# Places of tokens in extra sets worked out after the first list, and the last results loaded together on two queues

## The chip, the cores and the metric

The kernel runs on one core of one Trainium2 chip. The metric is the device time of one execution in microseconds (us). A core has five engines with an instruction stream each: PE (matrix products; its weight loads are shown as PEld), DVE (vector), ACT (activations), POOL (general, it also issues the indirect transfers) and SP (it issues most plain transfers). Data moves between HBM and the core's memory by DMA queues.

## What is computed

3125 tokens of 256 numbers and 50000 directed edges, sorted by their target, go through two layers, each a graph step and a mixture of experts. In each mixture every token goes to its two best experts of eight.

```python
# layer 1, graph: own features and those of the last edge into the node
agg = zeros_like(x).at[dst].set(x[src])
x = x + concat((xn, agg)) @ W.T + b          # xn: layernorm of x
# layer 1, experts: top 2 of 8, hidden size 1024
x = x + sum_over_two(weight_i * (relu(xn @ W1[e].T + b1[e]) @ W2[e].T + b2[e]))
# layer 2, graph: over all edges
msg = (t1[src] + (feat[src] * feat[dst]) @ W2) / sqrt(out_deg[src] * out_deg[dst])   # feat: layernorm of x, t1 = feat @ W1
x = x + unit_norm(leaky_relu(t1 + segment_sum(msg, dst)))     # 0 + ... for nodes with no edge in
# layer 2, experts: top 2 of 8, hidden size 256
x = x + xn + sum_over_two(weight_i * (gelu(xn @ w1[e] + b1[e]) @ w2[e] + b2[e]))
```

A token's two weights are the softmax over its two scores.

## The kernel before

Tokens lie in 25 tiles of 128 rows (the last holds 53), in two halves: tiles 0 to 13 and 14 to 24. X in the core's memory holds all of them.

**Routing.** `route_steps` (L649 to L777) is a generator: each `yield` hands the turn back to whatever it runs beside. It ranks a token's eight scores, marks the best and the two selected experts, and counts by two matmuls (L685, L686) how many tokens of each expert come before. From the counts it makes each token's place in its experts' list. An expert has a fixed set of tiles per half, with room for 488 or 368 tokens. A token over the room is given a place in an "extra set" further back: `extrai`, `extras`, `last` and `away` (L708 to L723) hold how many extra sets each expert needs and how far a place has to move, `past` (L731) marks the places over the room, and L735/L736 add `past` times `away`. Then r.at holds each token's two places (L740 to L745). The extra sets are used only in a branch that runs if some expert overflows.

`list_steps` (L779 to L863) turns places into lists: one-hot matrices `lane` and `col` on DVE, two passes of matmuls (L812) that count into PSUM, and from these `take` (which row to fetch) and `put` (where its result goes). Behind the list `route_steps` makes the two weights of each token (L759 to L776).

**Experts.** `experts` (L940 to L1088) goes through 16 sets, eight experts for each half. For one set: hidden chunks by matmuls into PSUM tile `big` (L1045) with an activation on ACT (L1049); then `turn` transposes the rows of the next set, gathered from a table by POOL (L999), into PSUM tile `tr`, of which there are two buffers (L1018), and DVE copies them out as `xs` (L1019); then the second matmuls into `y` (L1059), DVE adds the bias (L1064), and POOL scatters the result to `ytab` (L1068). Between these `slot()` gives one step to each generator of the list `beside`. The order of instructions on every engine is that in which this code issues them, under a manual schedule; so the number of yields in a generator sets where its work stands in each engine's order.

The route of the first half in layer 1 runs before the first `experts` call, beside the last of the graph step (`plus_own`). That of the second half runs inside it: `beside_first` (L1420) runs the rest of the graph step, the ranks, `route_steps(routed1[1], ...)`, then `windows` (L1137 to L1218) and `total_in`, `count_edges` (L1238), clears of tables, and the combine of the first half. `windows` finds where each tile's edges start: POOL numbers positions (L1144), DVE compares (`less`, L1153), PE counts (L1159), POOL fetches seven pieces `win` (L1168), a chain on DVE works on them (L1177 to L1208: `code`, `qf`, `same`, `into`), PE transposes `qf` and `code` into `tr` (L1216), and ACT copies them out as `qs` and `cs` (L1217).

**The end.** In layer 2 the results of the first half are loaded and combined beside the second half's sets (`beside_fourth`, L1764). For the second half, `one_result` loads result 0 or result 1 of groups of three tiles, all on SP's queue (L1747, L1751). Result 0 is loaded during the last set: the loads are declared free of the last set's scatters (`apart`), since in this half a token's result 0 is that of its lower-numbered expert, and the last expert's results are always result 1. Result 1 is loaded behind the last scatter. A combine is one DVE instruction for each tile and result (L1799), 11 of each; a group is stored as soon as its result 1 is added (`store`, L1118, on SP).

Of the kernel before, what the change touches and what calls it, by code (L numbers as in the profile page):

```python
# [8 lines left out]
F32 = mybir.dt.float32  # L9
F16 = mybir.dt.float16  # L10
BF16 = mybir.dt.bfloat16
I32 = mybir.dt.int32
AF = mybir.ActivationFunctionType
OP = mybir.AluOpType
# [86 lines left out]
def gnn_ffn_kernel(ctx: ExitStack, tc: tile.TileContext, x, src_a, src_d, dst_d, dst_row,  # L101
# [547 lines left out]
    def route_steps(r, rp, h, pl, layer, sc=None):  # L649
# [55 lines left out]
        nc.vector.tensor_scalar(stop, shift, room - 0.5, None, OP.add)  # L705
        nc.vector.tensor_sub(shift[:, 1:], shift[:, 1:], ends[:, :NE - 1])
        yield
        extrai = rp.tile([P, NE], I32, name="extrai")  # L708
        nc.vector.tensor_scalar(extrai, many, -room, 0.0, OP.add, OP.max)
        nc.vector.tensor_scalar(extrai, extrai, SX * P - 1, None, OP.add)  # L710
        nc.vector.tensor_scalar(extrai, extrai, (SX * P).bit_length() - 1, None, OP.arith_shift_right)
        if layer == 2:
            yield
        extras = rp.tile([P, NE], F32, name="extras")
        nc.vector.tensor_copy(extras, extrai)
        r.last = keep.tile([P, NE], F32, tag=f"last{layer}{h}", name="last")
        nc.vector.tensor_tensor_scan(r.last, ones_f[:, :NE], extras, 0.0, OP.mult, OP.add)
        r.over = r.last[0:1, NE - 1:]
        yield
        away = rp.tile([P, NE], F32, name="away")  # L720
        nc.vector.tensor_sub(away, r.last, extras)
        nc.vector.tensor_scalar(away, away, float(SX * P), FIXED[h] * P - 0.5, OP.mult, OP.add)
        nc.vector.tensor_sub(away, away, stop)  # L723
        if layer == 2:
            yield
        place = rp.tile([P, NE, n], F32, name="place")
        nc.vector.tensor_sub(place.rearrange("p e t -> p (e t)"), flat, count)
        nc.vector.tensor_add(place, place, pp[:, 0])
        yield
        nc.vector.tensor_add(place, place, shift[:, :, None].to_broadcast([P, NE, n]))  # L730
        past = rp.tile([P, NE, n], F32, name="past")  # L731
        nc.vector.tensor_tensor(past, place, stop[:, :, None].to_broadcast([P, NE, n]), OP.is_gt)
        if layer == 2:
            yield
        nc.vector.tensor_mul(past, past, away[:, :, None].to_broadcast([P, NE, n]))  # L735
        nc.vector.tensor_add(place, place, past)  # L736

        one = [best, rp.tile([P, n, NE], F32, name="second")]
        nc.vector.tensor_sub(one[1], sel, best)
        r.at = keep.tile([P, 2, n], F32, tag=f"at{layer}{h}", name="at")  # L740
        for i in range(2):
            yield
            got = rp.tile([P, n, NE], F32, name="got")
            nc.vector.tensor_mul(got, one[i], place.rearrange("p e t -> p t e"))
            nc.vector.tensor_reduce(r.at[:, i, :], got, AX.X, OP.add)  # L745
        yield

        r.weight = keep.tile([P, 2, n], F32, tag=f"weight{layer}{h}", name="weight")
        if t1 == T:
            none = rp.tile([P, 1], F32, name="none")  # L750
            nc.vector.tensor_scalar(none, real, -float(1 << 15), float(1 << 15), OP.mult, OP.add)
            nc.vector.tensor_scalar(r.at[:, :, n - 1], r.at[:, :, n - 1], none, None, OP.add)
        if not r.adds:
            yield from list_steps(r, rp, h, layer, 0, FIXED[h])
        if not softmax_first:
            sc.exps()
            yield
            yield
# [178 lines left out]
            nc.sync.dma_start(out=b2t, in_=b2[e, :].to_broadcast([P, D]))  # L937
            got += [w2, b2t]

    def experts(fp, sets, routed, tabs, weights, nh, act, beside=(), fresh=False, loaded=None, now=None,  # L940
                apart=None):


        lead = 2 if nh > 2 else 3
# [78 lines left out]
        with tc.manual_schedule(engines=ENGINES):  # L1023
# [10 lines left out]
            for k, (h, e, x) in enumerate(sets):  # L1034
# [20 lines left out]
                for j in range(n):  # L1055
                    m = last_rows if j == n - 1 else P
                    py = bank([P, D], F32, "y")
                    for c in range(nh):
                        nc.tensor.matmul(py[:m], hid[:, c, j * P:j * P + m], w2[:, c, :],  # L1059
                                         start=(c == 0), stop=(c == nh - 1))  # L1060
                        if c % 2 and c < nh - 1:
                            slot()
                    y = fp.tile([P, D], F32, name="y", bufs=4 if nh > 2 else 10)
                    nc.vector.tensor_add(y[:m], py[:m], b2t[:m])  # L1064
                    to = routed[h].column(c0 + j)
                    into = bass.IndirectOffsetOnAxis(ap=to[1][:m], axis=0)
                    if not routed[h].adds:
                        dma = nc.gpsimd.indirect_dma_start(  # L1068
                            out=tabs[h][1], out_offset=into, in_=y[:m], in_offset=None,
                            bounds_check=2 * tokens(h) - 1, oob_is_err=False)  # L1070
                        alone(dma, tabs[h][1], fresh)
                        if apart and k == len(sets) - 1:
                            tc.declare_no_dep(dma.ins, group=apart, reason="other rows")
                    else:

                        nc.scalar.activation(y[:m], y[:m], AF.Identity, scale=to[2][:m])
                        dma = nc.gpsimd.indirect_dma_start(
                            out=out, out_offset=into, in_=y[:m], in_offset=None,
                            bounds_check=N - 1, compute_op=OP.add)
                        tc.declare_no_dep(dma.ins, group=sums_of(h, e, x), reason="other rows")  # L1080
                        tc.add_to_no_dep_group(sums_of(h, e, x), dma.ins)
                    if nh > 2 or j % 2:
                        take(1)
                    slot()
# [30 lines left out]
            for t in range(t0, t1):  # L1115
                combine(h, r.weight_x if over else r.weight, y2, t0, t)

    def store(t0, t1):  # L1118
        whole = min(t1, T - 1)
        if whole > t0:  # L1120
            nc.sync.dma_start(out=out[t0 * P:whole * P, :].rearrange("(t p) d -> p t d", p=P), in_=X[:, t0:whole, :])
        if t1 == T:
            nc.sync.dma_start(out=out[(T - 1) * P:, :], in_=X[:LAST, T - 1, :])

# [439 lines left out]
    def to_the_end():  # L1566
# [171 lines left out]
            with tc.tile_pool(name="route3", bufs=1, reuse_waits="tile") as rp:  # L1738
                yield from route_steps(routed2[1], rp, 1, None, 2, state["scores"])

        def one_result(pool, t0, t1, i):

            first = HALVES[1][0]
            y1 = pool.tile([P, t1 - t0, D], F32, name=f"result{i}_{t0}")
            whole = min(t1, T - 1)
            ytab = tabs2[1][1]
            dmas = [nc.sync.dma_start(out=y1[:, :whole - t0],  # L1747
                                      in_=ytab[2 * (t0 - first) * P:2 * (whole - first) * P, :]
                                      .rearrange("(t p i) d -> p t i d", p=P, i=2)[:, :, i, :])]
            if t1 == T:  # L1750
                dmas.append(nc.sync.dma_start(out=y1[:LAST, T - 1 - t0],  # L1751
                                              in_=ytab[2 * (T - 1 - first) * P:, :]
                                              .rearrange("(p i) d -> p i d", i=2)[:, i, :]))
            return y1, dmas

        def beside_fourth():

# [3 lines left out]
            with tc.tile_pool(name="behind", bufs=1, reuse_waits="tile") as zp:  # L1761
                spans = groups(HALVES[0][1], 2)
                ahead = []
                for k in range(NE + 1, 2 * NE):  # L1764
# [2 lines left out]
                    due_now, ahead = ahead, []  # L1767
                    for t0, t1 in [spans.pop(0) for _ in range(min(len(spans), 2 if k == NE + 1 else 1))]:
                        ahead.append((t0, t1, results(zp, 0, tabs2[0][1], t0, t1, 3)))
                    if k == 2 * NE - 1:  # L1770
                        for t0, t1 in last_spans:
                            y1s.append(one_result(pools[0], t0, t1, 0))
                            for dma in y1s[-1][1]:
                                tc.add_to_no_dep_group("first results", dma.ins)
                    yield
                    for t0, t1, y2 in due_now:
                        for t in range(t0, t1):
# [3 lines left out]
                        yield  # L1781
                assert not spans and not ahead

        now2, y1s, pools, lasts = [0], [], [], ExitStack()
        last_spans = groups(T, 3, HALVES[1][0])
        experts(fp, fixed(0) + fixed(1), routed2, [tabs2[0], (placed, tabs2[1][1])], weights2, KD, AF.Gelu,
                [beside_third(), beside_fourth()], now=now2, apart="first results")
        over = small.tile([1, 1], F32, name="over2")
        nc.vector.tensor_add(over, routed2[0].over, routed2[1].over)
        over_i = small.tile([1, 1], I32, name="over_i")  # L1790
        nc.vector.tensor_copy(over_i, over)
        with tc.manual_schedule(engines=ENGINES):
            for i in range(2):
                if i:
                    y1s = [one_result(pools[0], t0, t1, 1) for t0, t1 in last_spans]
                for (t0, t1), (y1, _) in zip(last_spans, y1s):
                    for t in range(t0, t1):
                        n, c = P if t < T - 1 else LAST, t - HALVES[1][0]
                        nc.vector.scalar_tensor_tensor(X[:n, t, :], y1[:n, t - t0, :],  # L1799
                                                       routed2[1].weight[:n, i, c:c + 1], X[:n, t, :],  # L1800
                                                       OP.mult, OP.add)
                    if i:
                        store(t0, t1)
        lasts.close()
        aheads.close()

# [252 lines left out]
```

## Time and profile before

| | us |
|---|---|
| runs | 1065.77, 1068.58, 1069.88 (median 1068.58) |
| profiled execution | 1065.53 |
| its span (first to last instruction) | 1063.7 |
| PE busy | 955.2 |
| PE weight loads (beside PE) | 719.7 |
| DVE busy | 593.0 |
| ACT busy | 330.8 |
| POOL busy | 369.0 |

The mean granted clock of PE is 0.964 of full speed. Instructions on the engines overlap, so busy times don't add up to the span. A timeline line reads: start in us, busy us, engine, line of the code, operation, written tile<-read tiles, shape, number of instructions, and in brackets the idle time ahead of it and the instruction that ended it. A line `L1059` is a line of the kernel before. PE's busy time by stage, from windows of the trace:

| stretch (us) | PE busy | what runs |
|---|---|---|
| 0 to 100 | 68.1 | graph step of layer 1 |
| 100 to 151 | 29.6 | its end, route of the first half |
| 151 to 300 | 143.5 | experts of layer 1, windows beside them |
| 300 to 450 | 149.4 | experts of layer 1, counting of edges |
| 450 to 560 | 109.1 | the same, then the graph step of layer 2 |
| 600 to 700 | 98.1 | graph step of layer 2 |
| 700 to 800 | 97.0 | the same |
| 900 to 1000 | 89.1 | experts of layer 2 |
| 1000 to 1038 | 33.8 | the same |
| 1038 to 1063.7 | 0 | the last results |

### The profile page before, as it was taken

What the parts mean: (1) busy time and instruction counts of PE and PEld (TensorE: products, weight loads), DVE (VectorE), ACT (ScalarE), POOL (GpSimd) and SP (SyncE); (2) the same over time, 40 slices, a digit from 0 to 9 for tenths busy, and PEclk for the clock granted to TensorE, in tenths of its full rate; (3) what the DMA queues carried; (4) which work ended last, traced back from release to release, by engine and by line L of the source; (5) the groups of instructions that cost most, each with busy time, mean ns of one, the idle gap of its engine ahead of it and who ended that gap; (6) DMA issues with size and microseconds to landing.
All of it is one profiled execution on the core that took longest, in us unless ns stands there. A gap on an engine that the chain in (4) does not pass through costs nothing. (4 is left out here: it accounts for less than half of the span.)

```text
span 1063.7 us, 16259 instructions
## 1 busy us (share of the span) xinstructions
PE 955.2 (90%) x6057; PEld 719.7 (68%) x6057; DVE 593.0 (56%) x1544; ACT 330.8 (31%) x760; POOL 369.0 (35%) x393
## 2 busy tenths in 40 slices
PE   4678569998999999999999999999999999799990
PEld 4566446665667667777777788877888887566660
DVE  8966864773645555666564153633275344386563
ACT  2572421222335565666432111221111111312110
POOL 2867346422533213322332111011013245267450
PEclk9999779999999999999999999999999999899995
DMA  7675465533466958776653170601312024466875
GB/s 217 226 222 153 154 199 156 161 124 98 139 183 235 332 207 311 255 288 233 226 182 144 31 276 4 248 23 41 124 60 83 32 70 151 156 214 195 282 251 181
DMA packets 121584, 182.61 MB, mean 172 GB/s; under 512 B 20324, under 2 KB 97614, under 8 KB 121375
## 3 DMA queue, kind: packets, MB, share of 16 engines
q1 hardware_dynamic: 99459, 124.21, 35.4%
q0 software_dynamic: 13200, 34.14, 9.9%
q10 hardware_dynamic: 8836, 23.13, 5.8%
q8 instruction: 50, 0.82, 0.3%
q14 instruction: 39, 0.32, 0.1%
HBM read 108.30 MB, written 74.51 MB: 172 GB/s over the span
## 5 line engine op out<-in xcount | busy, mean ns | idle before, releaser
L1059 PE MATMUL y<-w,hid 128*128 128x256 f32 (+2 forms) x1120 | 270.1, 387 | 3.6 <-DVE y L1064 3.1
L1045 PE MATMUL big<-xs,w 128*128 128x488 f32 (+1 forms) x640 | 269.2, 544 | 0.9 <-ACT hid L1049 0.8
L1059 PEld LDWEIGHTS y<-w,hid 128*128 128x128 f32 (+2 forms) x1120 | 199.3, 187 | 34.5 <-DVE y L1064 6.8
L1712 PEld LDWEIGHTS <-at 128*128 128x128 bf16 x1875 | 183.7, 99 | 24.1
L1068 POOL DMA_INDIRECT ytab<-y,put x112 | 125.2, 1118 | 196.6 <-DVE y L1064 145.0
L1049 ACT ACTIVATE hid<-big,bt 128x488 f32<-128x488 f32 (+1 forms) x160 | 98.5, 617 | 211.6 <-PE big L1045 200.3
L1045 PEld LDWEIGHTS big<-xs,w 128*128 128x128 f32 x640 | 112.8, 194 | 61.1 <-issue 35.1
L1712 PE MATMUL big<-parts,at 128*128 128x256 bf16 x1200 | 145.0, 275 | 0.0
L999 POOL DMA_INDIRECT g<-xtab,take x56 | 61.0, 1090 | 145.0 <-PE tr L1018 105.5
L1064 DVE TENSOR_TENSOR y<-y,b2t 128x256 f32<-128x256 f32 (+1 forms) x112 | 47.0, 422 | 109.2 <-PE y L1059 108.2
L1268 PEld LDWEIGHTS <-hq 128*128 128x128 bf16 x800 | 57.3, 98 | 58.1 <-issue 38.3
L1248 DVE TENSOR_TENSOR hq<-qs,iota_b 128x2048 bf16<-128x2048 bf16 x50 | 61.2, 1223 | 55.7 <-PE sb L1268 55.7
L1019 DVE COPY xs<-tr 128x488 f32<-128x488 f32 (+1 forms) x64 | 35.8, 597 | 50.8 <-PE tr L1018 50.5
L1269 ACT CAST at<-sa 128x400 bf16<-128x400 f32 x100 | 49.0, 490 | 48.5 <-PE sa L1268 47.1
L1712 PE MATMUL sa<-parts,at 128*128 128x256 bf16 x525 | 62.2, 273 | 0.0
L1269 ACT CAST at<-sb 128x400 bf16<-128x400 f32 x100 | 49.0, 490 | 31.6 <-PE sb L1268 30.2
L1523 ACT COPY hT<-tr 128x512 f32<-128x512 f32 x25 | 14.4, 586 | 141.9 <-PE tr L1521 141.9
L1550 POOL TENSOR_TENSOR X<-X,kept 128x256 f32<-128x256 f32 x14 | 10.4, 771 | 122.6 <-DVE kept L512 122.6
L1109 DVE SCALAR_TENSOR_TENSOR X<-y,weight,X 128x256 f32<-128x256 f32 (+1 forms) x78 | 39.8, 532 | 20.8 <-DMA y<-ytab 19.8
L1251 DVE TENSOR_TENSOR hc<-cs,iota_b 128x1600 bf16<-128x1600 bf16 x50 | 49.2, 984 | 0.0
L1685 POOL DMA_INDIRECT xtab<-kept,place x28 | 27.6, 986 | 47.3 <-DVE place L1682 21.9
L1515 DVE SCALAR_TENSOR_TENSOR both<-big,deg,feat 128x256 f32<-128x256 f32 x16 | 7.7, 479 | 61.9 <-PE big L1712 61.8
(353 smaller groups left out, 1228.1 us busy)
## 6 DMA issues: line engine op xcount, KB each, us to landing
w<-in_fW SPq DMA_DIRECT2D x32, 1024.0 KB
atab<-at ACTq DMA_DIRECT2D x25, 800.0 KB
at<-atab SPq DMA_DIRECT2D x25, 800.0 KB
ytab<-zero_b SPq DMA_DIRECT2D x10, 1024.0 KB
y<-ytab SPq DMA_DIRECT2D x19, 512.0 KB
w<-in_mw SPq DMA_DIRECT2D x32, 256.0 KB
xtab<-zero_b SPq DMA_DIRECT2D x7, 1024.0 KB
rows<-xtab SPq DMA_DIRECT2D x8, 512.0 KB
```

The source lines that it names most:

```text
L999: nc.gpsimd.indirect_dma_start(out=g, out_offset=None, in_=tabs[h][0], in_offset=bass.IndirectOffsetOnAxis(ap=routed[h].column(c)[0], axis=0))
L1045: nc.tensor.matmul(ph[:, :many], w1[:, i, c * P:(c + 1) * P], turned[k][:, i, :many], start=(i == 0), stop=(i == KD - 1))
L1049: nc.scalar.activation(hid[:, c, :many], ph[:, :many], act, bias=bt[:, 0, c:c + 1])
L1059: nc.tensor.matmul(py[:m], hid[:, c, j * P:j * P + m], w2[:, c, :], start=(c == 0), stop=(c == nh - 1))
L1064: nc.vector.tensor_add(y[:m], py[:m], b2t[:m])
L1068: dma = nc.gpsimd.indirect_dma_start(out=tabs[h][1], out_offset=into, in_=y[:m], in_offset=None, bounds_check=2 * tokens(h) - 1, oob_is_er ...
L1109: nc.vector.scalar_tensor_tensor(X[:n, t, :], y2[:n, t - t0, i, :], weight[:n, i, i0:i0 + 1], X[:n, t, :], OP.mult, OP.add)
L1248: nc.vector.tensor_tensor(in_pairs(hq), pairs(qs[:, mine], P), in_pairs(iota_b[:, None, :].to_broadcast([P, n, P])), OP.is_equal)
L1251: nc.vector.tensor_tensor(in_pairs(hc), pairs(cs[:, mine], C), in_pairs(iota_b[:, None, :C].to_broadcast([P, n, C])), OP.is_equal)
L1268: nc.tensor.matmul(pa[:, j], hq[:, g + j, :], hc[:, g + j, :], start=True, stop=True)
L1269: nc.scalar.copy(at[:, :, W * (g0 + g):W * (g0 + g + 4)].rearrange("p i (g w) -> p i g w", w=W), pa.rearrange("p g i w -> p i g w"))
L1712: nc.tensor.matmul(sums[a][:, t - a, :], at[t][:, i, :], parts[:, i, k, :], start=False, stop=(i == T - 1 and k == 2 and t == b - 1))
```

## The change

Two parts that have nothing to do with each other.

**The route of layer 1.** The steps for the extra sets become a helper, `extra_steps`. In layer 1 ("late") a place over the room is first moved by a fixed 2^14, which puts it outside the fixed sets' list, in one instruction; at_steps and the list follow; then come `extra_steps`, the true distance less 2^14, the second addition to `place`, and `at_steps` once more, which makes r.at anew. In layer 2 the order stays, but for the subtraction that makes `second`.

**The last results.** `one_result` gives way to `last_results`: groups of two tiles instead of three, both results in one transfer (2 KB a row and tile instead of 1 KB), all behind the last scatter, alternately on SP's and ACT's queue. Each tile is then combined twice and its group stored, on alternate queues too. The declaration that parted the last set's scatters from the loads of result 0 goes.

```diff
         away = rp.tile([P, NE], F32, name="away")
+        def extra_steps():
+            extrai = rp.tile([P, NE], I32, name="extrai")
+            nc.vector.tensor_scalar(extrai, many, -room, 0.0, OP.add, OP.max)
+            nc.vector.tensor_scalar(extrai, extrai, SX * P - 1, None, OP.add)
+            nc.vector.tensor_scalar(extrai, extrai, (SX * P).bit_length() - 1, None, OP.arith_shift_right)
+            if layer == 2:
+                yield
+            extras = rp.tile([P, NE], F32, name="extras")
+            nc.vector.tensor_copy(extras, extrai)
+            r.last = keep.tile([P, NE], F32, tag=f"last{layer}{h}", name="last")
+            nc.vector.tensor_tensor_scan(r.last, ones_f[:, :NE], extras, 0.0, OP.mult, OP.add)
+            r.over = r.last[0:1, NE - 1:]
+            yield
+            nc.vector.tensor_sub(away, r.last, extras)
+            nc.vector.tensor_scalar(away, away, float(SX * P), FIXED[h] * P - 0.5, OP.mult, OP.add)
+            nc.vector.tensor_sub(away, away, stop)
+            if layer == 2:
+                yield
...
+        def at_steps():
+            for i in range(2):
+                yield
+                got = rp.tile([P, n, NE], F32, name="got")
+                nc.vector.tensor_mul(got, one[i], place.rearrange("p e t -> p t e"))
+                nc.vector.tensor_reduce(r.at[:, i, :], got, AX.X, OP.add)
+            if t1 == T:
+                none = rp.tile([P, 1], F32, name="none")
+                nc.vector.tensor_scalar(none, real, -float(1 << 15), float(1 << 15), OP.mult, OP.add)
+                nc.vector.tensor_scalar(r.at[:, :, n - 1], r.at[:, :, n - 1], none, None, OP.add)
+            yield
+
+        far = float(1 << 14)
+        late = layer == 1
+        if not late:
+            yield from extra_steps()
         nc.vector.tensor_sub(place.rearrange("p e t -> p (e t)"), flat, count)
         nc.vector.tensor_add(place, place, pp[:, 0])
         yield
         nc.vector.tensor_add(place, place, shift[:, :, None].to_broadcast([P, NE, n]))
         nc.vector.tensor_tensor(past, place, stop[:, :, None].to_broadcast([P, NE, n]), OP.is_gt)
         nc.vector.tensor_sub(one[1], sel, best)
+        if late:
+            nc.vector.scalar_tensor_tensor(place, past, far, place, OP.mult, OP.add)
+        else:
+            yield
+            nc.vector.tensor_mul(past, past, away[:, :, None].to_broadcast([P, NE, n]))
+            nc.vector.tensor_add(place, place, past)
+        yield from at_steps()
...
         if not r.adds:
             yield from list_steps(r, rp, h, layer, 0, FIXED[h])
+        if late:
+            yield from extra_steps()
+            nc.vector.tensor_scalar(away, away, -far, None, OP.add)
+            nc.vector.tensor_mul(past, past, away[:, :, None].to_broadcast([P, NE, n]))
+            yield
+            nc.vector.tensor_add(place, place, past)
+            yield from at_steps()
...
-                        if apart and k == len(sets) - 1:
-                            tc.declare_no_dep(dma.ins, group=apart, reason="other rows")
...
-    def store(t0, t1):
+    def store(t0, t1, queue=None):
+        queue = queue or nc.sync
...
-        def one_result(pool, t0, t1, i):
+        def last_results(pool, t0, t1, queue):
             first = HALVES[1][0]
-            y1 = pool.tile([P, t1 - t0, D], F32, name=f"result{i}_{t0}")
+            y2 = pool.tile([P, t1 - t0, 2, D], F32, name=f"result{t0}")
...
+            if whole > t0:
+                queue.dma_start(out=y2[:, :whole - t0],
+                                in_=ytab[2 * (t0 - first) * P:2 * (whole - first) * P, :]
+                                .rearrange("(t p i) d -> p t i d", p=P, i=2))
             if t1 == T:
+                queue.dma_start(out=y2[:LAST, T - 1 - t0],
+                                in_=ytab[2 * (T - 1 - first) * P:, :].rearrange("(p i) d -> p i d", i=2))
...
-                    if k == 2 * NE - 1:
-                        for t0, t1 in last_spans:
-                            y1s.append(one_result(pools[0], t0, t1, 0))
-                            for dma in y1s[-1][1]:
-                                tc.add_to_no_dep_group("first results", dma.ins)
...
-            for i in range(2):
-                if i:
-                    y1s = [one_result(pools[0], t0, t1, 1) for t0, t1 in last_spans]
-                for (t0, t1), (y1, _) in zip(last_spans, y1s):
...
+            y2s = [last_results(pools[0], t0, t1, nc.scalar if i % 2 else nc.sync)
+                   for i, (t0, t1) in enumerate(last_spans)]
+            for k, ((t0, t1), y2) in enumerate(zip(last_spans, y2s)):
+                for t in range(t0, t1):
+                    combine(1, routed2[1].weight, y2, t0, t)
+                store(t0, t1, nc.scalar if k % 2 else nc.sync)
```

## The prediction

> **What bounds the kernel now.** I read the page's busy shares first, then the chain of waits, then the timeline around each place that the diff touches, and windows of the throttle's grid.
>
> ```profile
> span 1063.7 us, 16259 instructions
> PE 955.2 (90%) x6057; PEld 719.7 (68%) x6057; DVE 593.0 (56%) x1544; ACT 330.8 (31%) x760; POOL 369.0 (35%) x393
> ...
> 1038.42 6.53 DMA ytab<-y,put
> 1046.96 6.45 DMA result<-ytab
> ```
>
> PE is the bound from about 150 to 1038 us: windows of PE give 149.4 of the 150 us from 300 to 450, 98.1 of 100 from 600 to 700. It is not the bound in the front (29.6 of the 51 us from 100 to 151), at the windows step (a 4.28 us stall at 238), and in the tail, where it has nothing after 1038 and the chain is two transfers. So the change counts at those three places; DVE work beside PE elsewhere is free.
>
> **Front, tokens of the first half, layer 1.**
>
> ```profile
> 130.53 0.16 DVE L709 TENSOR_SCALAR extrai<-many 128x8 int32<-128x8 f32 x1
> 131.96 0.17 DVE L723 TENSOR_TENSOR away<-away,stop 128x8 f32<-128x8 f32 x1
> ...
> 140.63 0.57 PE L812 MATMUL sa<-col,lane 128*128 128x64 bf16 x14 [1.53 <-DVE col L829]
> 142.83 0.94 POOL L999 DMA_INDIRECT g<-xtab,take  x1 [23.83 <-DVE high L636]
> 149.58 1.25 PE L1018 MATMUL tr<-ident,g 104*128 104x104 f32 x5 [0.93 <-DMA g<-xtab,take]
> 150.05 1.48 DVE L1019 COPY xs<-tr 128x488 f32<-128x488 f32 x2 [3.98 <-PE tr L1018]
> ```
>
> The eight small instructions L709–L723 leave the way of the list: they lie from 130.53 to 132.04, 1.5 us. The multiply and the add L735/L736 become one instruction, some 0.25 us less. DVE is then 1.75 us earlier at the one-hots. The first count can't follow: its column was ready at 138.48 and PE was busy with other work until 138.5 anyway. The second can, from 140.63 to 139.15, the end of the first: 1.5 us. List and four gathers follow (POOL issues one each 1.25 us from 142.83; all have landed at 149.58), and so does the first expert's matmul: −1.5.
> Eleven more DVE instructions stand behind the list, with the eight: 1.5 us and some 2.2 us for away−far, the product, the sum and the second pass of at_steps. Their cover is DVE's wait for the gathers (3.98 us before the xs copies). About 0.3 us of it is left by my addition; were it gone, the copies would come as late as before and the gain would be 0. Bounds: −2.5 (the first count moved too, with the half-clock stretch from 144.40 to 154.64 shortened) to 0. I take −1.5.
>
> **Middle, tokens of the second half, layer 1.** The same generator runs here beside the first layer's experts, one step per slot of PE's order. Before the list it is one slot shorter, behind the list it has extra_steps, away and at_steps again: four slots net, after which `windows` and everything in its order come four slots, four `big` matmuls of 0.82 us, later.
>
> ```profile
> 240.29 0.90 POOL L1144 IOTA w<- 128x896 int32 x1
> 242.40 0.33 PE L1159 MATMUL sa<-ones_b,less 128*128 128x1 bf16 x7 [4.28 <-DVE less L1153]
> ...
> 262.46 0.94 POOL L1168 DMA_INDIRECT win<-wtab,begin_i  x1 [19.79 <-issue]
> ...
> 284.90 0.60 PE L1216 MATMUL tr<-ident,qf 128*128 128x128 f32 x4
> 290.18 0.64 PE L1018 MATMUL tr<-ident,g 128*128 128x128 f32 x4 [0.70 <-ACT cs L1217]
> 292.33 1.23 DVE L1019 COPY xs<-tr 128x488 f32<-128x488 f32 x2
> ```
>
> First, a gain. PE's stall of 4.28 us waits for `less`, and that for POOL's numbering at 240.29. With 3.3 us more of PE's own work ahead of the first count, the stall falls to about 1. The granted clock, which was halved behind it, would stay up:
>
> ```profile
> 239.97:243.38 3.41, 0.98 (x9) 0.57 (x10) 2.12 (x5) 0.00 (x0) 2.53 (x3) 1.00 0.84 290
> 243.38:246.79 3.41, 3.41 (x19) 1.60 (x18) 1.13 (x3) 0.67 (x1) 0.00 (x0) 0.50 0.16 43
> ```
>
> (Columns: us, busy us of PE, its weight loads, DVE, ACT and POOL with instructions, granted clock, DMA share, GB/s.) The half-speed window does half its work, 1.7 us lost. PE is thus some 5 us ahead behind the counts.
> Then it is given back. The counted offsets go to POOL's seven gathers of `win` (from 262.46), then DVE's chain L1177–L1208, which ends with the `same` pairs at 292.4. That chain does not come earlier: the last count moves behind the transposes of the next set, and one more scatter and gather (2.5 us on POOL) stand ahead of `win`. I get 262.5 to 262.7 again. In DVE's order both xs copies stand behind all the `same` pairs, before and after; in PE's order the L1216 transposes of qf and code stood ahead of the next set's `tr<-g` and now stand behind it. Tile "tr" has two buffers: both `tr<-g` fill them, so the qf transposes wait for an xs copy, which waits for the chain. In before's order they waited only for qf and code, and L1018 for 0.70 us.
> In numbers: PE ends that set's `big` matmuls at about 282.5 and `tr<-g` at 283.5, 5 us ahead; the first xs copy ends at 293.1 (292.5 and 0.6). PE stands 9.6 us. Behind that are 2.2 us of transposes (14 of 0.15) and the 13.8 us of y matmuls: 309.1 to 309.6. Before, the same point (first one-hot matmul of count_edges) came at 305.97. The wait costs 3.0 to 3.6 in all, gains counted. Queued behind it on PE are the y matmuls, and on POOL their scatters and the next gathers; ACT's copies of cs wait too, with nothing due.
> The clock comes on top. 9.6 us of idle hold at least one whole window of 3.41 us. The trace halves the clock after such a window (0.98 us of work above) and restores it only after a full one, here from the front:
>
> ```profile
> 151.22:154.64 3.42, 3.42 (x5) 1.43 (x5) 3.32 (x12) 0.19 (x1) 2.51 (x4) 0.50 0.35 102
> 154.64:158.05 3.41, 3.41 (x9) 1.52 (x8) 1.75 (x6) 1.29 (x3) 2.50 (x4) 1.00 0.36 107
> ```
>
> PE restarts inside a window and needs the next one full: 3.4 to 6.8 us at half speed, 1.7 to 3.4 lost; I take 2.6. Middle: 3.0 to 3.6 and 2.6, **+6.2**; bounds +3.0 (clock kept) and +7.0, and −5.0 if the buffers came free in time.
> [...]
>
> **Tail.**
>
> ```profile
> 1044.96 1.96 SPq L1747 DMA_DIRECT2D result<-ytab  x4
> 1048.32 4.05 DVE L1799 SCALAR_TENSOR_TENSOR X<-result,weight,X 128x256 f32<-128x256 f32 x10 [1.80 <-DMA result<-ytab]
> 1053.50 0.48 DVE L1799 SCALAR_TENSOR_TENSOR X<-result,weight,X 53x256 f32<-53x256 f32 x1 [1.14 <-DMA result<-ytab]
> ```
>
> The last scatter is issued at 1038.42 and lands 6.53 us later, beside 1.4 MB of first results. With these gone, I take the landings of earlier scatters of the tile from 1030 on, 2.4 to 4.1 with a median of 3.0: −3.5 (bound 0). Then both results, 2.7 MB and 22 combines, come behind it instead of 11. From issue to first combine is 3.36 us before (1044.96 to 1048.32); with groups of twice the bytes I take 4.0 to 4.5: first combine at 1045.4 to 1045.9. 22 combines by 0.478 us are 10.5: the last ends between 1056 and 1057.3, before at 1053.98: +2.4 to +3.3. Alternating queues spread issues of 0.48 us each; on one queue the six groups' issues would lie beside the combines, so nothing for that (1.5 us, three issues, if they did not).
> The end has a second chain, stores behind loads:
>
> ```profile
> 1056.00:1057.00 1.00, 0.00 (x0) 0.00 (x0) 0.00 (x0) 0.00 (x0) 0.00 (x0) 0.50 0.07 24
> ```
>
> A share near 1/16 (0.10, 0.07, 0.10 in the three windows from 1055) is one or two engines of 16 working: the 53-row transfers, 54 KB in, 54 KB out, and a part of the others. At the 24 GB/s shown it moves its 133 KB of result 1 and 133 KB of stores in 11.1 us, from about 1047 to the 1058 seen. With both results it has 400 KB, 16.7 us, from about 1043.5: 1060.5, +2.4. Both ways agree; **+2.4** for the tail, bounds +1.0 (engine shared evenly) and +5.9 (the scatter lands no earlier). SP and ACT hold nothing else by then; layer 2's route only has one subtraction moved, beside PE.
> [...]
>
> **Sum:** −1.5 +6.2 +2.4 = +7.1. The profiled execution took 1065.5 us, so 1072.6 of the same kind; the median of the runs is 1068.58, so 1075.7.
>
> **Rivals.** (1) The other side: the xs copies come in time, because DVE's chain starts 9 us earlier or more. Then only the gain of the windows step shows: −1.5 −5.0 +2.4 = −4.1, 1064.5. For it: the counts really are earlier on PE; against it: `win` began with 19.79 us of POOL's own queue before it, and that queue has grown. 0.08. (2) The wait comes, the clock does not fall or recovers at once: middle +3.0, total +3.9, 1072.5. For it: in 243.38 the loss lasted one window alone. 0.2. (3) The last scatter lands as late as before, beside the stores of the first half, which no longer queue behind loads on SP: tail +5.9, total +10.6, 1079.2. 0.13. (4) The late list work on DVE delays the first xs copies: front 0, total +8.6, 1077.2. 0.05. The forecast itself 0.54, with its own range 1073 to 1079.
>
> **How the numbers follow.** 0.5% of 1068.6 is 5.3 us, about what a measurement can tell from none: faster needs under 1063.2, which rival 1 reaches in half its spread: 0.05. Within it lie the rest of rival 1, most of rival 2 and the forecast's low edge: 0.25. Slower: 0.70. The range drops rival 1 and the far half of 3: 1070.5 to 1080.
>
> **What would show it.** In the new profile: the transposes of qf with some 9 us idle ahead of them, put down to DVE's xs copy; the first `less` count with 1 us instead of 4.28; half clock in one or two windows from about 293; the first gather near 141.3; the last scatter landing in 3 to 4 us and 22 combines without gaps. If PE has no such wait ahead of qf, the forecast falls to rival 1.

## The result and the profile after

The changed kernel takes 1076.26 us (median of 16 runs, 1070.53 to 1080.9), the kernel before 1068.84 us (median of 16, 1065.77 to 1072.36). The ratio is 1.0067 with a 95% interval of 1.0051 to 1.0083: slower by 7.4 us between the medians, 5.5 to 8.9 by the interval. The forecast was 1075.7 with a range of 1070.5 to 1080. The profiled execution took 1076.88 us.

The page and the chain of waits of the changed kernel:

```profile
span 1075.2 us, 16263 instructions
PE 955.2 (89%) x6057; PEld 719.9 (67%) x6057; DVE 597.9 (56%) x1558; ACT 331.2 (31%) x760; POOL 368.7 (34%) x393
...
1045.65 2.40 DMA ytab<-y,put
...
1048.07 6.42 DMA result<-ytab
```

PE's busy time is the same to the tenth of a microsecond, the span 11.5 us longer: what grew is idle time. The last scatter lands in 2.40 us instead of 6.53. The timeline of the changed kernel at the front and at the windows step (L1017, L1176, L1036, L1223, L1233 and L1037 are the former L999, L1159, L1018, L1206, L1216 and L1019):

```profile
139.44 0.94 POOL L1017 DMA_INDIRECT g<-xtab,take  x1 [20.93 <-DVE extrai L712]
146.54 1.48 DVE L1037 COPY xs<-tr 128x488 f32<-128x488 f32 x2
...
238.56 0.33 PE L1176 MATMUL sa<-ones_b,less 128*128 128x1 bf16 x7 [1.01 <-DVE less L1170]
...
278.70 1.00 PE L1036 MATMUL tr<-ident,g 128*128 128x128 f32 x8
...
287.84 0.63 DVE L1223 TENSOR_SCALAR same<-w 128x896 f32<-128x896 f32 x1
289.50 1.23 DVE L1037 COPY xs<-tr 128x488 f32<-128x488 f32 x2
290.21 1.11 PE L1233 MATMUL tr<-ident,qf 128*128 128x128 f32 x4 [10.51 <-DVE xs L1037]
```

Read from the bottom: PE stood 10.51 us ahead of the qf transposes, until the first xs copy had ended at 290.2. The copy itself came late, since DVE still had the `same` pairs ahead of it. The stall ahead of the first `less` count has shrunk from 4.28 to 1.01 us. Windows of the changed kernel, 3.41 us each and set so that the changes of the granted clock (at 283.25 and 293.49) fall on their edges, with the columns of the windows above:

```profile
279.83:283.25 3.42, 0.00 (x0) 0.00 (x0) 3.32 (x5) 0.00 (x0) 0.80 (x1) 0.99 0.91 312
283.25:286.66 3.41, 0.00 (x0) 0.00 (x0) 3.31 (x4) 0.00 (x0) 0.00 (x0) 0.50 0.10 34
286.66:290.08 3.42, 0.00 (x0) 0.00 (x0) 3.32 (x6) 0.00 (x0) 0.00 (x0) 0.50 0.00 0
290.08:293.49 3.41, 3.27 (x12) 2.81 (x13) 0.65 (x2) 1.01 (x1) 0.00 (x0) 0.51 0.13 4
293.49:296.90 3.41, 3.41 (x21) 3.00 (x20) 0.00 (x0) 2.56 (x3) 0.00 (x0) 1.00 0.53 9
```

Behind the first idle window the clock is 0.50; work came back at the very start of the window at 290.08, and from 293.49 on the clock is 1.00: one window of work at half speed, by half of 3.41 us some 1.7 us lost. The tail of the changed kernel:

```profile
1048.07 2.57 SPq L1765 DMA_DIRECT2D result<-ytab  x3
1048.07 1.67 ACTq L1765 DMA_DIRECT2D result<-ytab  x2
...
1054.52 10.15 DVE L1125 SCALAR_TENSOR_TENSOR X<-result,weight,X 128x256 f32<-128x256 f32 x22 [10.00 <-DMA result<-ytab]
...
1064.75 0.27 ACTq L1140 DMA_DIRECT2D out<-X  x1
```

The first combine starts 6.45 us behind the first load's issue (3.36 before); then 22 of them run without a gap.

**A ledger by intervals.** The starts of work differ from trace to trace, so I measure each part from an event just ahead of it. Front: from the route's count matmul (L685) of the first half to the first set's xs copies. Middle: from the second set's xs copies to the eighth's, around the windows step. Later: from there to the last scatter of layer 1. Layer 2: on to its last scatter's issue. Tail: from that to the end of the span. The experiments ran on three chips: on that of e1 to e4 the kernel before takes 1147.21 us, on that of e5 to e8 1141.44 us, on that of e9 to e12 1069.09 us. Ratios are against the runs of before on the same chip, and a time in us that stands beside a ratio is worked out from it. The intervals come from one profiled execution each; the rows of before and changed are those of the profiles above.

| kernel | front | middle | later | layer 2 | tail |
|---|---|---|---|---|---|
| before | 21.28 | 193.13 | 247.59 | 431.20 | 25.28 |
| changed | 19.55 | 197.70 | 249.83 | 435.66 | 29.55 |
| e1 route alone | 19.50 | 198.73 | 249.56 | 468.12 | 26.88 |
| e2 tail alone | 21.26 | 200.20 | 247.59 | 461.98 | 28.92 |
| e3 four slots | 21.37 | 194.77 | 250.67 | 471.38 | 26.03 |
| e4 same slots | 19.64 | 201.39 | 247.59 | 470.04 | 25.59 |
| e5 four slots again | 21.35 | 197.83 | 251.21 | 461.37 | 26.89 |
| e6 first half late | 19.35 | 199.33 | 247.59 | 466.16 | 25.44 |
| e7 one queue | 21.41 | 199.69 | 247.58 | 470.43 | 26.97 |
| e8 windows later | 19.51 | 187.75 | 262.43 | 461.13 | 25.83 |
| e9 early numbers | 19.68 | 186.96 | 247.60 | 432.26 | 25.91 |
| e10 last tile split | 21.27 | 194.01 | 247.59 | 435.51 | 22.41 |
| e11 all three | 19.38 | 187.47 | 247.59 | 433.31 | 22.62 |
| e12 changed again | 19.47 | 197.82 | 252.11 | 426.41 | 29.34 |

### The profile page after: what moved, and what is told of

The parts are those of the page before. It is cut to its first block, busy times and chain, and to the rows that moved or that the text cites. A ratio compares the mean times of both kernels' runs of the same rounds, so it can differ in the third digit from the quotient of the medians.

```text
span 1075.2 us, 16263 instructions
## 1 busy us (share of the span) xinstructions
PE 955.2 (89%) x6057; PEld 719.9 (67%) x6057; DVE 597.9 (56%) x1558; ACT 331.2 (31%) x760; POOL 368.7 (34%) x393
## 5 line engine op out<-in xcount | busy, mean ns | idle before, releaser
L1729 PE MATMUL big<-parts,at 128*128 128x256 bf16 x1200 | 147.4, 277 | 0.0
L1017 POOL DMA_INDIRECT g<-xtab,take x56 | 59.8, 1069 | 136.6 <-PE tr L1036 100.0
L1037 DVE COPY xs<-tr 128x488 f32<-128x488 f32 (+1 forms) x64 | 35.7, 597 | 47.9 <-PE tr L1036 47.5
```

The lines of the kernel that those rows point to most:

```text
L1017: nc.gpsimd.indirect_dma_start(out=g, out_offset=None, in_=tabs[h][0], in_offset=bass.IndirectOffsetOnAxis(ap=routed[h].column(c)[0], axis=0))
L1729: nc.tensor.matmul(sums[a][:, t - a, :], at[t][:, i, :], parts[:, i, k, :], start=False, stop=(i == T - 1 and k == 2 and t == b - 1))
```

## The experiments

**e1, the route alone.** The diff's `route_steps` with the tail of before.

> The change's route alone, with the last results loaded as before. My theory (the sum is front, middle and tail): the profile has the front of the changed kernel (xs copies of the first set 3.5 us earlier than before), the wait of some 10 us ahead of the qf transposes, and a tail as before; time +0.5 to +3 us over before (front -3.5, middle +4.6 to +6.2). Rival A (the tail alone makes the slowdown): -3 to 0 us. Rival B (nearly all is the middle, and the front gain is chance): +4 to +7 us.

Ratio 0.9997 (0.9970 to 1.0024): no difference that can be told; by the time alone this is what rival A expected on this chip. The front is 1.8 us shorter than in the kernels without the late route, and the wait ahead of qf is there, but 4.90 us long. The timeline of e1's PE:

```profile
309.98 1.90 PE L1064 MATMUL big<-xs,w 128*128 128x488 f32 x4 [2.17 <-issue]
...
314.13 1.91 PE L1064 MATMUL big<-xs,w 128*128 128x488 f32 x4 [2.25 <-issue]
...
317.00 6.81 PE L1064 MATMUL big<-xs,w 128*128 128x488 f32 x16 [0.96 <-ACT hid L1068]
329.55 1.11 PE L1235 MATMUL tr<-ident,qf 128*128 128x128 f32 x4 [4.90 <-DVE xs L1038]
```

On this chip PE stands still for 2.17 and 2.25 us in the `big` matmuls ahead, for nothing that the profile shows ("issue"). It reaches the qf transposes late, and DVE's chain goes on meanwhile: the wait is what is left of it. Counted over "middle" and "later", e1, e3 and e5 (new order) take 445.4 to 449.0 us and e2, e4, e6 and e7 (old order) 446.9 to 449.0: on the two slower chips the new order costs nothing that these intervals show.

**e2, the last results alone.** The diff's tail with the route of before.

> The change's last results alone, with the route as before. My theory: +2.4 to +4.5 us: from the issue of the last scatter to the end of the span 28 to 29.6 us instead of 25.3, with the scatter landing in 2.4 to 3 us, the first combine 6 to 6.5 us behind the loads' issue and 22 combines of 0.48 us. Rival A (the tail alone makes the slowdown): +6 to +8 us. Rival C (the tail is even): -1 to +1 us.

Ratio 1.0038 (1.0011 to 1.0065), +4.4 us. The tail is 28.92 us against 25.4 to 26.9 in the kernels of the two slower chips with the tail of before; the scatter lands in 2.39 us. The first combine came 4.8 us behind the issue, earlier than the 6 that I expected here. The last two combines then waited for the 53-row load, which landed 12.85 us behind its issue:

```profile
1131.95 0.99 DVE L1106 SCALAR_TENSOR_TENSOR X<-result,weight,X 53x256 f32<-53x256 f32 x2 [1.08 <-DMA result<-ytab]
```

**e3, four empty slots.** The kernel before and nothing but:

```diff
+            for _ in range(4):
+                yield
             yield from windows()
```

> The kernel before with four empty yields ahead of windows in beside_first, and nothing else: no instruction is added. My theory (PE's order and the two tr buffers make the wait, not the added DVE work): the first less count waits 1 us instead of 4.3, PE waits 9 to 11 us ahead of the qf transposes on an xs copy, the clock is halved for one or two windows around it; time +3 to +6 us over before. Rival (DVE's 19 added route instructions make the chain late): no wait of over 2 us ahead of the qf transposes, and -5 to 0 us.

Ratio 0.9988 (0.9960 to 1.0016). Not the +3 to +6 that I expected; the wait was 1.65 us, under the 2 us that the rival allowed, so this run by itself speaks for the rival. The timeline of e3's PE:

```profile
277.34 0.33 PE L1159 MATMUL sa<-ones_b,less 128*128 128x1 bf16 x7 [1.01 <-DVE less L1153]
312.02 3.42 PE L1045 MATMUL big<-xs,w 128*128 128x488 f32 x4 [4.21 <-issue]
316.89 8.45 PE L1045 MATMUL big<-xs,w 128*128 128x488 f32 x20 [1.45 <-ACT hid L1049]
327.83 0.66 PE L1216 MATMUL tr<-ident,qf 128*128 128x128 f32 x4 [1.65 <-DVE xs L1019]
```

The stall ahead of `less` is 1.01 as in the changed kernel, with no added instruction; of the wait there is little, behind standstills of 4.21 and 1.45 us and four matmuls that took 3.42 us (1.90 us for four in e1).

**e4, the route in the same slots.** All the late DVE work, but in the second half issued at one point, so that every engine's order around windows is that of before:

```diff
-        if late:
+        if late and h == 0:
+            yield from late_steps()
+        elif late:
+            for _ in late_steps():
+                pass
+            yield
```

(late_steps is the diff's block behind the list.)

> The change's route, with its added steps of the second half issued in one slot, so that windows stands in every engine's order where it stood before; the tail as before. All of the added DVE work is there. My theory: no wait ahead of the qf transposes, the stall of 4.3 us ahead of the first less count is back, time -2 to -4 us against before (the front gain alone). Rival (the added DVE work makes the middle's loss): the wait or an equal one on DVE appears, 0 to +4 us.

Ratio 0.9986 (0.9963 to 1.0008), inconclusive as a time. The trace is not (timeline of e4, L1184 and L1241 are the former L1159 and L1216):

```profile
280.53 0.34 PE L1184 MATMUL sa<-ones_b,less 128*128 128x1 bf16 x7 [6.21 <-DVE less L1178]
...
329.89 0.60 PE L1241 MATMUL tr<-ident,qf 128*128 128x128 f32 x4
```

There is no wait ahead of qf, "later" is 247.59 us to the hundredth as before, and the stall ahead of `less` is back, 6.21 us instead of the 4.28 and 4.29 of e2, e6 and e7 with the old order on these chips. The added instructions now stand in one piece ahead of it on DVE. So the added work costs 1.9 us there, and not in the way of the change.

**e5, four slots again.** The kernel of e3 once more.

> The same kernel as in the run with four empty yields: the kernel before, with four empty yields ahead of windows. In that run PE had stood still for other reasons (4.2 us in which it waited for nothing that the profile shows, in the big matmuls ahead of the transposes), so it reached the qf transposes late. My theory: where PE has no such standstill, it waits 9 to 11 us ahead of the qf transposes on an xs copy, and the time is +3 to +6 us over before; where it has one of 4 us or more, the wait is what is left (1 to 5 us) and the time -1 to +2 us. Rival (the wait comes from the added DVE work): no wait of over 2 us in either case.

Ratio 1.0007 (0.9972 to 1.0041). PE's standstills here are smaller, and the wait is larger:

```profile
309.17 1.90 PE L1045 MATMUL big<-xs,w 128*128 128x488 f32 x4 [1.30 <-ACT hid L1049]
...
315.47 8.50 PE L1045 MATMUL big<-xs,w 128*128 128x488 f32 x16 [2.33 <-ACT hid L1049]
329.44 1.11 PE L1216 MATMUL tr<-ident,qf 128*128 128x128 f32 x4 [4.63 <-DVE xs L1019]
```

Without one instruction added, a wait of the same kind as the changed kernel's appears, on the same copy: its cause is the order. The rival (added DVE work) falls, by this run together with e4. The full 10.5 us appear in none of e1, e3 and e5, which all ran on the slower chips; the order alone was not run on a chip of 1069 us.

**e6, the first half late.** The diff's route with `late = layer == 1 and h == 0`, slots of the second half as before, old tail.

> The change's route for the first half alone (late only where h is 0; the second half's order, yields and slots as before), the tail as before. My theory: the front gain stands by itself, xs copies of the first set 1.5 to 3.5 us earlier than before and nothing given back: -1.5 to -4 us. Rival (the front gain is eaten by the next wait or by chance of the clock windows): -1 to +1 us.

Ratio 0.9999 (0.9970 to 1.0027): the time can't tell 1.8 us here. The interval can: the front is 19.35 us against 21.26 to 21.41 in e2, e3, e5 and e7 without it, and nothing is given back in "middle" or "later".

**e7, the new tail on one queue.** The tail of e2 with `nc.sync` for every load and store.

> The change's last results with all loads and stores on SP's queue (groups of two tiles, both results in one transfer, all behind the last scatter), route as before. Theory A (two queues make the groups share the transfer engines, so that the first group lands late): the first combine comes 3.5 to 4.5 us behind the first issue instead of 4.8 to 6.5, the last combine 1 to 2 us earlier than with two queues, and the time is 0.5 to 2 us under that kernel's +4.4 us. Theory B (22 combines of 0.48 us and the last tile's transfers set the end, not the queues): within 0.7 us of it. Theory C (the issues of 0.48 us each on one queue cost): 1 to 3 us over it.

Ratio 1.0004 (0.9977 to 1.0031). The tail is 26.97 us, 1.95 less than on two queues in e2, which ran on another chip. The timeline of e7:

```profile
1120.84 3.37 SPq L1746 DMA_DIRECT2D result<-ytab  x5
...
1125.07 9.25 DVE L1106 SCALAR_TENSOR_TENSOR X<-result,weight,X 128x256 f32<-128x256 f32 x20 [7.77 <-DMA result<-ytab]
1135.56 0.99 DVE L1106 SCALAR_TENSOR_TENSOR X<-result,weight,X 53x256 f32<-53x256 f32 x2 [1.24 <-DMA result<-ytab]
```

From issue to first combine 4.23 us, against 4.82 in e2: that is theory A's sign. But the last combine ends only 0.4 us earlier, counted from the scatter's issue, not 1 to 2; the other 1.5 us lie behind it, of which theory A says nothing. With one profile each, two chips and ratios that overlap, it stays open whether one queue is better.

**e8, windows later.** e6 with 16 empty slots ahead of windows.

> The first half's late route as in the run with the first half alone, and 16 empty yields ahead of windows, so that the xs copies stand ahead of most of DVE's chain and the qf transposes among y matmuls that PE can do first. My theory: neither the stall ahead of the first less count (4.3 us) nor the wait ahead of qf is there, the clock stays up in this stage, and the time is 3 to 6 us below that of the run with the first half alone. Rival (DVE's y additions now wait behind the chain's wait for win, and PE behind them): a wait of 3 us or more at y matmuls, and no gain over that run.

Ratio 0.9979 (0.9953 to 1.0004). The middle is 11.6 us shorter than in e6, and "later" 14.8 us longer: by these intervals more than all is given back. PE waited 4.4 us at y matmuls as the rival said, and then, where the combine of the first half now falls, this (timeline of e8):

```profile
563.40 1.92 DVE L1129 SCALAR_TENSOR_TENSOR X<-y,weight,X 128x256 f32<-128x256 f32 x4 [9.68 <-DMA y<-ytab]
...
567.24 6.67 PE L1065 MATMUL big<-xs,w 128*128 128x368 f32 x12 [7.56 <-ACT hid L1069]
```

ACT's part of the combine stands in its order ahead of the activations that PE needs, and DVE's part waits for a load.

**e9, early numbers.** e6, with POOL's numbering and its copy taken out of windows:

```diff
+                first = ip.tile([P, GW * P], F16, name="first")
                 with tc.tile_pool(name="route", bufs=1, reuse_waits="tile") as rp:
+                    firsti = rp.tile([P, GW * P], I32, name="firsti")
+                    nc.gpsimd.iota(firsti, pattern=[[W, GW * P]], base=0, channel_multiplier=0)
                     sc = Scores(rp, 1, pre[:, n:])
                     yield from sc.ranked(0, T - n)
+                    nc.vector.tensor_copy(first, firsti)
...
-                yield from windows()
+                yield from windows(first)
```

> The first half's late route as in the run with the first half alone, every slot as before, and POOL's numbering of positions with its copy moved out of windows to the ranks of the second half, so that the first less count need not wait for it. My theory (the stall ahead of less is a wait for POOL and nothing that the later chain needs): the 4.3 us stall is 1 us or less, the clock stays up behind it, the copies of the second set behind the windows come 2 to 5 us earlier counted from the first set's, and the time is 2 to 5 us under that of the run with the first half alone. Rival (PE, once ahead, waits for qf and code instead, as in the changed kernel): the stall reappears ahead of the qf or code transposes with 3 us or more, and the gain is under 1.5 us.

Ratio 0.9918 (0.9885 to 0.9950), −8.8 us, from six runs. The stall ahead of `less` is 0.16 us, no new one has come ahead of qf or code, and the middle is 6.2 to 7.1 us shorter than in before and e10, more than the 2 to 5 that I expected of it. The timeline of e9:

```profile
236.65 0.33 PE L1175 MATMUL sa<-ones_b,less 128*128 128x1 bf16 x7 [0.16 <-DVE less L1169]
...
282.87 0.64 PE L1038 MATMUL tr<-ident,g 128*128 128x128 f32 x4 [0.70 <-ACT cs L1233]
```

Here the counts come earlier, so POOL's `win` and DVE's chain do too: the first `win` is issued 90.3 us behind the second set's xs copies, against 96.0 in before (262.46 less 166.50) and 96.3 in the changed kernel (258.76 less 162.46). PE and DVE stay in step. That is what the change didn't do: it moved PE's work ahead of the chain, not the chain.

**e10, the last tile split.** The kernel before, with the 53-row result loads and store in two parts:

```diff
-            nc.sync.dma_start(out=out[(T - 1) * P:, :], in_=X[:LAST, T - 1, :])
+            for a, b in ((0, 48), (48, LAST)):
+                nc.sync.dma_start(out=out[(T - 1) * P + a:(T - 1) * P + b, :], in_=X[a:b, T - 1, :])
```

> The kernel before, with the transfers of the last tile's 53 rows at the end cut into 48 and 5 rows (its result loads and its store). Theory A (the tail's end is one transfer engine that carries all 53-row transfers): from the issue of the last scatter to the end of the span 2 to 4 us less than the 25.4 to 26.9 of the kernels with the tail of before, and no stretch of 3 us with a DMA share near 1/16. Theory B (the combines and the fixed end set it): within 0.7 us.

Ratio 0.9965 (0.9948 to 0.9982), −3.7 us; the tail is 22.41 us against 25.28 in before and 25.91 in e9. Windows of e10 at its end:

```profile
1058.00:1059.00 1.00, 0.00 (x0) 0.00 (x0) 0.00 (x0) 0.00 (x0) 0.00 (x0) 0.50 1.03 343
1059.00:1060.00 1.00, 0.00 (x0) 0.00 (x0) 0.00 (x0) 0.00 (x0) 0.00 (x0) 0.50 0.48 123
1060.00:1061.00 1.00, 0.00 (x0) 0.00 (x0) 0.00 (x0) 0.00 (x0) 0.00 (x0) 0.50 0.02 4
```

The DMA share is 1.03 from 1058 to 1059, 0.48 in the next microsecond and then 0.02; the stretch of three microseconds with 0.07 to 0.10 (before, 1055 to 1058) is gone. Both signs that theory A named are there; on how many engines the 53-row transfers ran, no run shows.

**e11, all three.** e9 with the split of e10.

> The first half's late route, the early numbering and the split last tile together, nothing else of the change. My theory: the sum of the three, -4 to -9 us against before. If the parts cover one another or one is worth nothing, -1.5 to -4 us.

Ratio 0.9852 (0.9819 to 0.9884): 1053.93 us, −15.8 us. It beats both kernels, by more than the sum that I expected. The intervals account for some 11 (front 1.9, middle 5.7 to 6.5, tail 2.7 to 3.3), and that is all of the profiled execution: at 1058.19 us it is 10.9 under the median of before. The rest lies between runs: three of the six took 1057.4 to 1058.2 us at a granted clock of 0.961 to 0.963, three 1049.2 to 1050.5 us at 0.968 to 0.969. None of the last three was profiled, so their cause stays open.

**e12, the changed kernel again.**

> The changed kernel itself, on the chip of the experiments. My theory from the parts measured by intervals of the traces: front -1.8 us (from the counts of the route to the first xs copies), middle -3 us where PE has its standstill of some 4 us in the big matmuls ahead of qf (+4.6 us where it has none), +2 to +3.6 us between there and the last scatter of layer 1, tail +2.8 to +4.3 us: with the standstill 0 to +3 us in all, without it +7 to +10 us. Rival (the loss doesn't depend on the standstill): +6 us or more with it.

This chip had no standstill, and the wait is back in full (timeline of e12):

```profile
293.00 1.12 PE L1233 MATMUL tr<-ident,qf 128*128 128x128 f32 x4 [10.63 <-DVE xs L1037]
```

Ratio 1.0058 (1.0035 to 1.0080), +6.2 us (3.7 to 8.6; the medians are 4.8 apart), at the low end of the +7 to +10 that I expected there or under it. The rival needed a run with the standstill, so this run doesn't test it.

## Why the prediction was right

**Front, −1.5.** Measured −1.6 to −2.1: 19.35 to 19.68 us in the eight traces with the late route, 21.26 to 21.41 in those without. The cover was tight as worked out: in the changed kernel the xs copies follow DVE's last late instruction without idle time, so another microsecond of late work would have counted. The prediction counted eleven added instructions behind the list; the trace has seven beside the eight, and all fifteen lie within 3.8 us (138.94 to 142.78) where 3.7 were taken. The 3.5 us by which the first copies come earlier in absolute time is partly chance: the count matmul itself started 1.78 us earlier, and nothing of the change lies ahead of it.

**Middle, +6.2.** The mechanism is shown: the order makes the wait (e3 and e5, with no work added), and the work without the order does not (e4). Its size here rests on the traces of the changed kernel, where order and work come together. The stall ahead of `less` was to fall to 1: 1.01. The wait was to be 9.6: 10.51 and 10.63. The clock's loss was to be 2.6: some 1.7, one window (3.27 us of work in it were enough, where I took a full one to be needed); and +6.2 takes the upper end of the prediction's own 3.0 to 3.6 for the wait. Up to the eighth set the two traces of the changed kernel are 3.7 to 4.7 us longer than those of before and e10. 16 matmuls of `count_edges` lie behind that mark now instead of ahead of it, 0.9 to 1.1 us; with them it is 4.6 to 5.8, a little under the forecast.
What I put at nothing makes up for it: four slots later for `count_edges` and the combine. "Later" is 247.59 us to the hundredth or two in every kernel with the old slots and 249.56 to 252.11 with the new ones (e8 apart). In the changed kernel it is 2.2 us longer (4.5 in e12); 0.9 and 1.1 of that are the 16 matmuls, the rest is PE waiting. A part of the waiting is this, in the changed kernel's timeline:

```profile
424.43 0.49 ACT L1286 CAST at<-sa 128x400 bf16<-128x400 f32 x1 [2.69 <-DMA atab<-at]
...
424.97 0.34 PE L1285 MATMUL sa<-hc,hq 128*128 128x100 bf16 x4 [1.62 <-ACT at L1286]
```

ACT finds a buffer of `at` not yet stored, and PE finds the bank not yet copied (1.6 us, 1.5 in e12). The rest is PE waiting for `hid` where the combine starts (2.8 us in all in e12, 0.5 in the changed kernel's first trace, 0.8 in before), the mechanism that e8 shows large. So the middle in all is +5.9 to +9.2 rather than +6.2: a smaller clock loss and a term of 1.3 to 3.5 that I left out. That +6.2 is in this range is partly luck.

**Tail, +2.4.** The direction and the first chain are right; the size is off. The scatter was to land 3.5 us earlier: 4.1. Between issue and first combine I took 4.0 to 4.5 us: 6.45 and 6.64. That term, "with groups of twice the bytes", is the mis-sized one; why it is 4.8 in e2 with the same loads stays open. 22 combines took 10.15 us instead of 10.5. The prediction's sum doesn't close either: 1045.4 to 1045.9 and 10.5 give 1055.9 to 1056.4, which is +1.9 to +2.4 and not +2.4 to +3.3. The tail grew by 3.4 to 4.3 us, so that the +2.4 is 1 to 2 us short, within its bounds. The second chain, the 53-row transfers, bounded the kernel before, as e10 shows (22.41 us with them split, 25.28 without); that one engine carries them was an estimate from the DMA share near 1/16. In the changed kernel the combines run without a gap to 1064.7 and the last store can start only then, so there the combines bound it; but the second chain is close behind, since in e2 and e7, where the first combine came sooner, the last two waited 1.1 and 1.2 us for the 53-row load.

**The sum.** By the intervals, front, middle, later and tail add up to +7 to +12 us, the runs say +7.4 (5.5 to 8.9) and +6.2 (3.7 to 8.6). The 11.5 us between the two profiled spans hold 4.5 us of layer 2, and these are not the change's: in before, changed, e10 and e12 PE does the same 2859 matmuls there and is idle for the same 22.8 to 23.0 us, while its busy time goes from 403.5 us (e12, granted clock 0.99) to 412.8 (changed, 0.96), and e10, with the old route and the old order of loads, has 412.7. The profile of e12 has one stretch at half clock in that stage, those of changed and e10 have four. That the total came out within 1 us of the forecast is in part luck: the front 0.1 to 0.6 us better, the tail 1 to 2 us worse, a smaller clock loss against a term left out.

Of the rivals, the other side (buffers free in time) fell, on the chips of 1069 us and on the others. The late landing of the scatter did not happen, and the late list work did not hold up the first copies. The shorter clock loss is partly what came. What I had not priced is PE's own lateness: on the two chips where PE stands still ahead of the transposes, the wait shrinks to 1.6 to 4.9 us, and the route alone costs nothing that can be measured.

## What to carry to other kernels

A generator's empty step is not free where its steps set the order of several engines: four more yields moved transposes behind others that hold both buffers of a PSUM tile, and tied PE to the end of a DVE chain. Before moving work off a short path, list what stands behind it in each engine's order, and who holds the buffers there; to gain, move the start of the chain that the wait hangs on (e9), not the work in front of it. The transfers of a ragged last tile can be worth splitting: here 53 rows as 48 and 5 took the tail from 25.28 to 22.41 us (e10).

## What the runs showed of the hardware that I had not expected

The same kernel takes 1069 us on one chip and 1141 and 1147 us on two others. On the chip of 1147 us PE has standstills of 2.17 and 2.25 us (e1) and 4.21 us (e3) that the profile puts down to "issue" rather than to an engine or a transfer; their cause stays open. The granted clock was 0.50 behind a window of 3.41 us that held no PE work at all (changed kernel, 279.83) and behind one with 0.98 us of it (before, 239.97), but 1.00 behind one with 1.55 us (before, 236.56). Where work returned at a window's start (changed kernel, 290.08), the clock was 1.00 again after that one window, 3.27 us busy; behind a window with 2.12 us (before, 147.81) it was still 0.50.
